# A two-layer conditioned block on one core: LayerNorms of blocks 4 to 7 asked for sooner, one product of the ff residual plain in two blocks, one block's statistics on VectorE, rounds of leaves moved

## The chip, the cores and the metric

The kernel runs on one core of a Trainium2 chip. The metric is device time in microseconds of one execution; the median over several runs is compared. One execution was recorded by the hardware profiler, and all rows of the profile below come from it.

## What is computed

The input is x (2 batches of 2048 tokens of 512 features) and a condition vector per batch. Cut to what matters, the reference is:

```python
emb = silu(t) @ ada_w + ada_b
shift_msa, scale_msa, gate_msa, shift_mlp, scale_mlp, gate_mlp = split(emb, 6)
norm = ln(x) * (1 + scale_msa) + shift_msa
h = gelu(norm @ ssm_w1 + ssm_b1)                  # 512 x 512
x = x + gate_msa * (h @ ssm_w2 + ssm_b2)          # 512 x 512
norm2 = ln(x) * (1 + scale_mlp) + shift_mlp
hf = gelu_tanh(norm2 @ ff_w1 + ff_b1)             # 512 x 1024
x = x + gate_mlp * (hf @ ff_w2 + ff_b2)           # 1024 x 512
```

All of it is fp32.

## The kernel before

The 4096 tokens are cut into 8 blocks of 512. In the first half of the program the blocks run one by one through norm1 (LayerNorm, transposed, modulated), ssm1 (first product with its gelu), ssm2 (second product, gated residual) and norm2 (LayerNorm of the result, transposed, kept in DRAM). In the second half they run in pairs s = 0 to 3: ff1 s for two blocks at once, then ff2 for each of them.

**Products by seven.** Every large product is done by Strassen's scheme in Winograd's form: the operands are cut into quarters, sums of quarters are formed on VectorE and POOL (`first`, `second`, L420 and L430), and seven products P1 to P7 take the place of eight; the results are added up in PSUM and by VectorE. One product of ssm1 or ssm2 (`product`, L771) is four matmuls of 256 columns. ff1 uses the scheme twice, one inside the other. In ff2 and in parts of ssm2 some of the seven products are themselves done by seven smaller ones, called leaves: a leaf of ff2 is two matmuls of 128 columns, a leaf of ssm2's head one. A product that isn't cut in leaves is called plain here.

**The head of ssm2 and its rounds.** P1 and P5 of ssm2 are done by leaves, and ahead of the rest: their matmuls stand between the products of the next block's ssm1. `head` (L697) makes four rounds. Round 0 seeds two PSUM banks with the bias, runs the leaves P1 and P5 of both products, and has ScalarE copy the results aside; round 1 runs leaves P6 and P2 and has VectorE add; round 2 runs P7 and has VectorE add; round 3 runs P4 and P3. With round 1 go two sums that later leaves need (`with_late`, L760). `HEAD_AT` (L694) names the products of ssm1 behind which the rounds stand. ssm1's own order is `CARRIED` (L445): P1, P5, P6, P2, P7, P3, P4. There are six such heads, for blocks 1 to 6, in ssm1 2 to ssm1 7; block 7's head stands in ssm2 6 and has its own list, `LAST_HEAD_AT`.

**P6 of ff2.** In ff2 (`ff2`, L1114) P6 is done by leaves if its leaf operands are among `wops` (`sixth`, L1211: four steps spread over the chain's rounds, with ScalarE copies, POOL adds and VectorE adds beside 14 matmuls), and else in one piece in chain round 4 (`plain_sixth`, L1204: eight matmuls of 256 columns). `fw2_sixth` (L934) makes the weight's leaf operands by four sums, one of which overwrites a quarter of the plain operand.

**norm1.** `norm1` (L629) loads a block of x (1 MB), takes mean and variance (`stats`, L516, on VectorE), makes the scales by eight small operations on POOL (`scales`, L551), normalises on ScalarE and transposes on VectorE in four slices through two small buffers, writes the transposed rows to DRAM in four DMAs, loads them back rearranged in one (blocks 3 to 7), modulates them on ScalarE in four pieces, and forms the four sums that ssm1 needs (`norm1_sums`, on VectorE or POOL). Blocks 4 to 7 are asked for in the loop at L1417, three blocks ahead.

**norm2's statistics.** For the blocks in `STATS_BY_ACT` (L526), norm2 takes the statistics on ScalarE, by eight activations with an accumulated sum (`act_sum`, L528); for the others by `stats` on VectorE.

**Who sets the order.** Nothing is issued where it is written. Each operation goes into a planner (`Plan`, from L20) with the engines that may do it, a cost and a latency. TensorE's operations keep the order in which they are written. Each gets a due time by summing their costs; from these a latest time (`late`) is worked out backwards for every other operation:

```python
late = min(late, ops[s].late - (1 + op.care) * (self.HOP + min(op.lat.values()) + op.size / self.RATE))
```

Here HOP is 70 ns and RATE 370 bytes per ns. `care` is the value of `plan.care` when the operation was added. Then the planner simulates the engines: each takes, of the operations whose inputs are there, the one with the earliest latest time. A large DMA is taken to land after

```python
pipe = max(start + self.FLIGHT, pipe) + op.size / self.RATE * (1 + self.RATED * op.care)
op.end = pipe + self.LANDING + self.LANDED * op.care
```

with RATED 0.5 and LANDED 4000 ns. The order that comes out is fixed when the kernel is built: each engine, and SP's DMA queue, works through its own list and waits at the head of it. So an edit of a latest time can reorder every engine's list. Almost all DMAs are issued on SP's queue.

Of the kernel before, what the change touches and what calls it, by code (L numbers as in the profile page):

```python
# [198 lines left out]
def kernel(  # L199
# [35 lines left out]
    plan = Plan(nc)  # L235
# [287 lines left out]
            plan.add("v", lambda E, st=st, dst=dst: E.bn_aggr(dst, st), [dst], [st], {"v": 100}, {"v": 182})  # L523
        return t, mv

    STATS_BY_ACT = (2, 4, 5)  # L526

    def act_sum(o, a, func, total, bias, scale):  # L528
        ptrs = [] if isinstance(bias, float) else [bias]
# [69 lines left out]
    def next_blocks():  # L599
        turns[0] += 1  # L600
        return blocks[turns[0] % 2]
# [9 lines left out]
    def normed(src, dst, bl, by_act=False):  # L611
        t, mv = stats_by_act(src, banks[2]) if by_act else stats(src)
        rstd, nmr = scales(t, mv)
        for c in range(C):
            normal(dst, src, c, rstd, nmr)
            turn(bl, dst, c)
        return cut(bl, "p (m r) -> p m r", m=C)
# [7 lines left out]
    def turned_out(to, bl):  # L625
        for a in range(C):
            dma(to[:, a].rearrange("(m q) r -> q m r", m=C), bl[a * G : (a + 1) * G])

    def norm1(i):  # L629
        plan.stage = f"norm1 {i}"  # L630
        load_x(i)
        bl = normed(xs[i], passing, next_blocks())
        if i in turned1_d:
            turned_out(turned1_d[i], bl)
            dma(turned[i], turned1_d[i])
        else:
            move(turned[i], bl)
        for k in range(KD):
            modulate(turned[i], k, 0, i // PER_B)
        return norm1_sums(i)  # L640
# [38 lines left out]
    def norm2(i):  # L679
        plan.stage = f"norm2 {i}"  # L680
        turned_out(turned_d[i], normed(xs[i], passing if i else xs[i], next_blocks(), i in STATS_BY_ACT))

# [8 lines left out]
        stages[0] += 1  # L691
        return bank_set()

    HEAD_AT, LAST_HEAD_AT = ("P5", "P2", "P7", "P3"), ("P6", "P2", "P7", "P3")  # L694
    SECOND_BY_LEAVES = (1, 2, 3, 4, 5, 6, 7)

    def head(stage, leaves, seeds, at=HEAD_AT):  # L697
# [41 lines left out]
    def second_leaves(wops):  # L739
        plan.stage = "leaves of w2"  # L740
        return {p: second(halves_of(wops[p]), w2_l[n]) for n, p in enumerate(("P1", "P5"))}

    def second_head(i, ops):
        if i not in SECOND_BY_LEAVES:
            return {}
        plan.stage = f"ssm2 {i}"
        row, leaves = gb2[i // PER_B], {}
        lates = []
        for n, p in enumerate(("P1", "P5")):
            still = first(crossed(ops[p]), hidden_l[i >= PER_B][n])  # L750
            lates.append(still)
            leaves[p] = lambda f, p=p, still=still: (still[f], w2_leaves[0][p][f])

        def seeds(n, bank):
            copy(bank[:, HT:], row[:, n * HT : (n + 1) * HT])

        at = LAST_HEAD_AT if i + 1 == NBLK else HEAD_AT
        rounds = head(f"ssm2 {i}", leaves, seeds, at)

        def with_late(fn):  # L760
            fn()
            for o in lates:
                tt("vg", o["P2"], o["P2"], o["P6"], ALU.subtract)

        rounds[at[1]] = lambda fn=rounds[at[1]]: with_late(fn)
        return rounds
# [71 lines left out]
    def ssm2(i, ops, wops, order=CARRIED, hooks={}):  # L838
        plan.stage = f"ssm2 {i}"
        b = next_set()  # L840
        row = gb2[i // PER_B]
        xt, F = xs[i], D // 2
        q = {"P2": xt[:, 0:2, :F], "P6": xt[:, 0:2, F:], "P3": xt[:, 0:2, F:], "P4": xt[:, 2:4, :F]}
        q["P1"], q["P5"] = q["P2"], xt[:, 2:4, F:]
        q["P7"] = q["P5"]
        if i in SECOND_BY_LEAVES:
            order = AFTER_HEAD
            copy(pair(b["x"]), pair(b["y"]))
            tt("v", q["P5"], pair(b["v"]), q["P5"], ALU.add)
        else:  # L850
            seed(b["y"], row, 0)
            seed(b["v"], row, 1)
        for p in order:
            product(
                b[BANK[p]],
                p,
                lambda j, k: ops[p][:, k, j * P : (j + 1) * P],
                lambda j, k: wops[p][:, k, :],
                KD // 2,
                p == "P2" and order is PLAIN,  # L860
            )
            if p == "P1" and order is CARRIED:
                copy(pair(b["x"]), pair(b["y"]))
            else:
                tt("v", q[p], pair(b[BANK[p]]), q[p], ALU.add)
            between(hooks, p, f"ssm2 {i}")
        for h in range(2):
            dma(x1_d[i][:, 2 * h : 2 * h + 2], xt[:, 2 * h : 2 * h + 2])
# [6 lines left out]
    def quarter_row(b):  # L875
        t = cut(gb2[b], "p (h e d) -> p h e d", h=2, e=2)
        tt("vg", t[:, :, 1], t[:, :, 1], t[:, :, 0], ALU.subtract)

    def weight2(b, bank):
        plan.stage = f"weight2 {b}"  # L880
        t = w2_t[b]
        load_w(t, w2)
        g = gate(2, b, bank)
        gate_bias(gb2[b], g, b2)
        for k in range(KD):
            tt("v", t[:, k, :], t[:, k, :], g, ALU.mult)
        return second(quarters_of_second(t, KD), thirds(w2_s), cuts=1)
# [33 lines left out]
    def leaves_of(w, at):  # L921
        return second({n: v[:, :, 0, :] for n, v in leaf_views(w).items()}, thirds(fw2_l[:, at]))
# [11 lines left out]
    def fw2_sixth(plain, leaves):  # L934
        leaves["P6"] = leaves_of(plain, 6)

    def weight_fw2(b, bank):
        plan.stage = f"weight_fw2 {b}"
        for n in range(2):
            for o in range(2):  # L940
                dma(fw2_t[:, 4 * n + 2 * o : 4 * n + 2 * o + 2], fw2_source()[n, o], lead=100000.0)
        g = gate(5, b, bank)
        gate_bias(gb5, g, fb2)
        for n in range(2):
            lo, hi = [gb5[:, (2 * n + e) * P : (2 * n + e + 1) * P] for e in range(2)]
            tt("vg", hi, hi, lo, ALU.subtract)
        for k in range(KH):
            tt("v" if bank else "vg", fw2_t[:, k, :], fw2_t[:, k, :], g, ALU.mult)
        return fw2_operands()
# [29 lines left out]
    def weight_fw2_loaded(b):  # L979
        plan.stage = f"weight_fw2 {b}"  # L980
        for n in range(4):
            dma(fw2_t[:, 2 * n : 2 * n + 2], fw2_d[:, 2 * n : 2 * n + 2])
        for n in range(3):
            dma(fw2_s[:, n], fw2_sd[:, n])
        load_row(gb5, gb5_d)
        q, t = quarters_of_second(fw2_t, KH), thirds(fw2_s)
        return fw2_operands({"P1": q["11"], "P2": q["21"], "P3": q["22"], "P4": t[2], "P5": t[0], "P6": t[1], "P7": q["12"]})
# [14 lines left out]
    def normed2(i):  # L1002
        plan.stage = f"tokens {i}"
        t = turned2[i % 2]
        if i in SOON:
            for a in range(C):
                dma(t[:, a], turned_d[i][:, a])
        else:
            dma(t, x1_d[i])
            move(t, normed(t, t, kb(far_r, 0, 8)))  # L1010
        for k in range(KD):
            modulate(t, k, 3, i // PER_B)
# [403 lines left out]
    weight_fw1()  # L1416
    for i in range(1, NBLK):  # L1417
        if i + 3 < NBLK:
            plan.care = 0.2
            tok[i + 3] = norm1(i + 3)  # L1420
            plan.care = 0.45
        last = i + 2 >= NBLK
        hooks = second_head(i + 1, hid[i + 1]) if last and i + 1 < NBLK else {}
        ssm2(i, hid[i], w2_ops, CARRIED, hooks)
        if i in SOON:
            norm2(i)
        if i == 4:
            ff = weight_fw2(0, 1)
            fw2_sixth(*ff)
        if i + 1 == PER_B:  # L1430
            w2_ops = weight2(1, 1)
            quarter_row(1)
            w2_leaves[0] = second_leaves(w2_ops)
        if not last:
            hid[i + 2] = ssm1(i + 2, tok[i + 2], w1_ops, second_head(i + 1, hid[i + 1]))
    for s in range(NBLK // 2):
        if 2 * s == PER_B:
            ff = weight_fw2_loaded(1)
            fw2_sixth(*ff)
        if 2 * s + 2 == PER_B:  # L1440
            weight_fw2_ahead(1)
        ff1(s)
        if 2 * s + 2 < NBLK and 2 * s + 2 not in SOON:
            normed2(2 * s + 2)
        for blk in range(2):
            ff2(s, blk, *ff)
# [51 lines left out]
```

## Time and profile before

| what | value |
|---|---|
| median of 3 runs | 568.27 us (567.67 to 569.56) |
| the profiled execution | 569.21 us, of which its span 567.4 us |
| ssm1 4 begins (norm1 4 needed) | 107.48 us |
| ssm1 7 begins (norm1 7 needed) | 180.19 us |
| ff1 0 begins | 216.7 us |
| ff2 0 and ff2 1 | 259.4 to 303.4 us |

Rows name a line (L294 is the matmul of `mm`, L256 the two-tensor operation of `tt`, L274 an activation, L283 a copy on ScalarE, L316 a DMA), the engine, the operation and the tiles written and read. The tiles are named by their regions: `turned` holds transposed tokens, `hidden` ssm1's and ff1's results, `rows`, `ring` and `far` blocks of x among others, `near` weights, `fw` ff weights, `bank` PSUM. PE is TensorE, PEld its weight loads, DVE VectorE, ACT ScalarE, POOL GpSimd, SPq the queue of DMAs. Since the program's order is known, a row can be matched to its stage.

### The profile page before, as it was taken

The page shows a single profiled execution, that of the slowest core. Times are in us where ns is not written, and L with a number is a line of the kernel's source. Part 1 is how long each engine was busy: PE and PEld are TensorE (multiplying, and loading weights), DVE is VectorE, ACT ScalarE, POOL GpSimd, SP SyncE. Part 2 cuts the span into 40 slices and gives each one's busy share as a digit, 9 for nine tenths or more (in the row PEclk, how much of TensorE's full clock was granted, in tenths as well). Part 3 has the DMA queues.
Part 4 walks back from the last instruction along what each step waited for, and adds up shares of the span by engine and source line. Part 5 has one row for each costly group of instructions (what it writes and reads, how often), then busy time and mean ns, then how long its engine had stood idle before and what let it go on. Part 6 is the DMA issues. An engine that isn't in the chain of part 4 may idle for free.

```text
span 567.4 us, 10428 instructions
## 1 busy us (share of the span) xinstructions
PE 559.0 (99%) x3577; PEld 506.5 (89%) x3577; DVE 489.0 (86%) x918; ACT 271.8 (48%) x558; POOL 384.1 (68%) x523
## 2 busy tenths in 40 slices
PE   8999999899999999999999999999999999999997
PEld 4888889788897988889999889999889999888997
DVE  5696988799886988989989889999999898789785
ACT  3464856777685875659112356222266222335120
POOL 2887547598934598994767897667795685446660
PEclk9999999999999999999999999999999999999999
DMA  8954899987899867896054889168955041820022
GB/s 314 399 217 90 246 360 277 320 299 264 258 310 307 270 217 220 276 317 217 20 186 152 304 279 342 68 205 274 319 174 207 2 150 43 273 93 29 1 75 74
DMA packets 53057, 119.85 MB, mean 211 GB/s; under 512 B 5473, under 2 KB 10509, under 8 KB 51470
## 3 DMA queue, kind: packets, MB, share of 16 engines
q1 hardware_dynamic: 51842, 118.66, 62.6%
q8 instruction: 28, 0.46, 0.4%
q10 hardware_dynamic: 1164, 0.55, 0.3%
q14 instruction: 23, 0.19, 0.1%
HBM read 77.63 MB, written 40.51 MB: 208 GB/s over the span
## 4 chain that ended last, share of the span: by engine, by line
PE 89%; DMA 6%; DVE 2%; ACT 1%; SPq 1%; issue 0%; DVEq 0%; ACTq 0%
PE bank L294 89%; DMA turned<-turned 3%; DMA turned<-far 2%; DMA fw<-in_L_cond_ada_w_dram 1%; SPq L316 1%; DVE far L591 1%; PE bank L304 0%; DVE rows L256 0%; ACT hidden L274 0%; ACT turned L274 0%; ACT near L274 0%; DVE marks L522 0%; ACT bank L283 0%; DVE ring L256 0%; DVE turned L656 0%
## 5 line engine op out<-in xcount | busy, mean ns | idle before, releaser
L294 PE MATMUL bank<-turned,ring 128*128 128x256 f32 x896 | 209.1, 380 | 1.2 <-ACT turned L274 1.0
L294 PEld LDWEIGHTS bank<-turned,ring 128*128 128x128 f32 x896 | 167.3, 190 | 24.8 <-ACT turned L274 1.8
L256 DVE TENSOR_TENSOR hidden<-bank,hidden 128x512 f32<-128x512 f32 (+1 forms) x171 | 124.8, 755 | 26.9 <-PE bank L294 23.5
L294 PE MATMUL bank<-near,hidden 128*128 128x256 f32 (+1 forms) x470 | 95.6, 350 | 1.8 <-DVE rows L256 1.8
L294 PEld LDWEIGHTS bank<-near,hidden 128*128 128x128 f32 x470 | 82.1, 190 | 11.8 <-DVE rows L256 2.6
L294 PE MATMUL bank<-fw,hidden 128*128 128x128 f32 x640 | 91.0, 276 | 0.0
L256 DVE TENSOR_TENSOR rows<-bank,rows 128x128 f32<-128x128 f32 (+3 forms) x154 | 78.8, 555 | 9.4 <-PE bank L294 8.8
L294 PE MATMUL bank<-ring 128*128 128x256 f32 x336 | 82.5, 381 | 0.0
L294 PEld LDWEIGHTS bank<-fw,hidden 128*128 128x128 f32 x640 | 81.3, 192 | 0.5
L283 ACT COPY bank<-bank 128x512 f32<-128x512 f32 (+2 forms) x88 | 37.2, 424 | 78.0 <-PE bank L294 77.2
L294 PEld LDWEIGHTS bank<-ring 128*128 128x128 f32 x336 | 63.2, 190 | 10.9 <-issue 2.1
L256 POOL TENSOR_TENSOR turned<-turned 128x512 f32<-128x512 f32 (+1 forms) x58 | 63.8, 1114 | 13.2 <-ACT turned L274 6.7
L294 PE MATMUL bank<-fw,far 128*128 128x128 f32 (+1 forms) x656 | 67.4, 275 | 0.1
L256 POOL TENSOR_TENSOR hidden<-hidden 128x128 f32<-128x128 f32 (+2 forms) x52 | 45.6, 881 | 28.8 <-DVE hidden L256 13.5
L274 ACT ACTIVATE hidden<-hidden,cols 128x512 f32<-128x512 f32 (+1 forms) x66 | 44.9, 711 | 38.4 <-DVE hidden L256 38.3
L294 PEld LDWEIGHTS bank<-fw,far 128*128 128x128 f32 (+1 forms) x656 | 61.2, 168 | 1.7 <-issue 1.3
L294 PE MATMUL bank<-fw,near 128*128 128x128 f32 x464 | 61.0, 275 | 0.0
L294 PEld LDWEIGHTS bank<-fw,near 128*128 128x128 f32 x464 | 56.4, 192 | 0.0
L256 POOL TENSOR_TENSOR fw<-fw 128x256 f32<-128x256 f32 (+1 forms) x51 | 42.0, 838 | 14.8 <-DVE turned L256 7.9
L274 ACT ACTIVATE turned<-turned,mod,mod 128x512 f32<-128x512 f32 x56 | 41.9, 805 | 15.5 <-DMA turned<-turned 14.8
L256 DVE TENSOR_TENSOR hidden<-hidden 128x512 f32<-128x512 f32 (+2 forms) x58 | 37.7, 665 | 1.9 <-POOL hidden L256 1.3
L256 POOL TENSOR_TENSOR ring<-turned,ring 128x256 f32<-128x256 f32 x40 | 29.7, 752 | 12.4 <-PE bank L294 6.4
(141 smaller groups left out, 710.2 us busy)
## 6 DMA issues: line engine op xcount, KB each, us to landing
ring<-fw_parts SPq DMA_DIRECT2D x28, 512.0 KB
turned<-far SPq DMA_DIRECT2D x52, 256.0 KB
ring<-fw_parts SPq DMA_DIRECT2D x28, 384.0 KB
rows<-x SPq DMA_DIRECT2D x32, 256.0 KB
turned<-turned SPq DMA_DIRECT2D x32, 256.0 KB
out_dram<-rows SPq DMA_DIRECT2D x28, 256.0 KB
fw_parts<-fw SPq DMA_DIRECT2D x21, 256.0 KB
fw<-in_L_cond_ada_w_dram SPq DMA_DIRECT2D x5, 1024.0 KB
```

The source lines that it names most:

```text
L256: lambda E: E.tensor_tensor(o, a, b, f),
L274: lambda E: E.activation(o, a, func, bias=bias, scale=scale),
L283: plan.add("a", lambda E: E.copy(o, a), [o], [a], {"a": cost}, {"a": cost + 60})
L294: lambda E: E.matmul(o, lhsT, rhs, start=start, stop=stop, skip_group_check=True, **kw),
L316: plan.add(q, lambda E: E.dma_start(out=o, in_=a), outs, ins, {q: plan.ISSUE}, {q: lat}, size=size, lead=lead)
L591: plan.add("v", lambda E: E.transpose(o, a), [o], [a], {"v": 636}, {"v": 705})
```

## The change

Four things are edited:

- Block 2 leaves `STATS_BY_ACT`: its norm2 statistics go from ScalarE to VectorE.
- `HEAD_AT` becomes P5, P6, P2, P3: rounds 1 and 2 of the six heads stand behind P6 and P2 of ssm1 in place of P2 and P7; rounds 0 and 3 stay behind P5 and P3.
- The operations of norm1 4 to norm1 7 are added with a care of 0.45 in place of 0.2.
- `fw2_sixth` for the first batch is called ahead of s = 1 in place of block 4's turn in the first half. So ff2 0 and ff2 1 find no leaf operands for P6 and do it plain; the leaf operands are made later, for ff2 2 and ff2 3.

```diff
-    STATS_BY_ACT = (2, 4, 5)
+    STATS_BY_ACT = (4, 5)
...
-    HEAD_AT, LAST_HEAD_AT = ("P5", "P2", "P7", "P3"), ("P6", "P2", "P7", "P3")
+    HEAD_AT, LAST_HEAD_AT = ("P5", "P6", "P2", "P3"), ("P6", "P2", "P7", "P3")
...
         if i + 3 < NBLK:
-            plan.care = 0.2
+            plan.care = 0.45
             tok[i + 3] = norm1(i + 3)
             plan.care = 0.45
...
         if i == 4:
             ff = weight_fw2(0, 1)
-            fw2_sixth(*ff)
...
     for s in range(NBLK // 2):
+        if s == 1:
+            fw2_sixth(*ff)
         if 2 * s == PER_B:
             ff = weight_fw2_loaded(1)
             fw2_sixth(*ff)
```

## The prediction

> **What bounds the kernel now.** I read the page's busy times, then what TensorE waited for, then the two longest of those waits in the timeline and in the chain of work that ended last. The page first: its columns are busy time, share of the span, instructions.
>
> ```profile
> span 567.4 us, 10428 instructions
> PE 559.0 (99%) x3577; PEld 506.5 (89%) x3577; DVE 489.0 (86%) x918; ACT 271.8 (48%) x558; POOL 384.1 (68%) x523
> ```
>
> TensorE is busy 99% of the span, so the change can win only what TensorE waits, and pays in full for any matmul time it adds. All its waits, with their releasers (total, times, longest):
>
> ```profile
> PE bank L294 <- DVE rows L256: 1.8, 2, 1.5
> PE bank L294 <- POOL small L321: 1.3, 1, 1.3
> PE bank L294 <- ACT turned L274: 1.0, 1, 1.0
> PE bank L294 <- DVE turned L656: 0.2, 1, 0.2
> ```
>
> The POOL and L656 rows are the start of the kernel, which no edit touches. The two others are single events. The timeline around them (start, duration, engine, operation, count; in brackets the idle time before it and who ended it):
>
> ```profile
> 99.69 4.48 PE L294 MATMUL bank<-near,hidden 128*128 128x256 f32 x20
> ...
> 103.70 0.69 DVE L256 TENSOR_TENSOR turned<-turned 128x512 f32<-128x512 f32 x1 [2.93 <-ACT turned L274]
> 104.31 1.28 DVE L256 TENSOR_TENSOR rows<-bank,rows 128x512 f32<-128x512 f32 x2
> ...
> 105.65 1.99 PE L294 MATMUL bank<-near,hidden 128*128 128x256 f32 x8 [1.48 <-DVE rows L256]
> ```
>
> ```profile
> 170.39 8.80 PE L294 MATMUL bank<-near,hidden 128*128 128x256 f32 x40
> ...
> 180.19 2.05 PE L294 MATMUL bank<-turned,ring 128*128 128x256 f32 x7 [1.01 <-ACT turned L274]
> ...
> 180.90 1.16 PEld L294 LDWEIGHTS bank<-turned,ring 128*128 128x128 f32 x6 [0.41 <-ACT turned L274]
> ```
>
> The pace of TensorE between waits (every matmul leaves two records, so x16 is two products of four matmuls):
>
> ```profile
> 107.48 3.62 PE L294 MATMUL bank<-turned,ring 128*128 128x256 f32 x16
> 110.93 0.38 PE L294 MATMUL bank<-near,hidden 128*128 128x128 f32 x2
> ...
> 111.83 3.62 PE L294 MATMUL bank<-turned,ring 128*128 128x256 f32 x16
> ```
>
> Eight matmuls of 256 columns take 110.93 - 107.48 = 3.45 us, 0.431 each. So the 10 matmuls from 99.69 would have been followed at 104.00; they were at 105.65: **1.65 us lost**. The 20 from 170.39 end at 179.01, the next came at 180.19, 1.18 lost, and the weight load of the second pair, due at 180.62, started at 180.90, 0.28 more: **1.46 us lost**. Whose fault? At 103.70 a sum of the LayerNormed tokens (turned<-turned) stood at the head of VectorE's queue and waited 2.93 us for ScalarE's modulation; the evictions (rows<-bank) that TensorE needed stood behind it. That block is norm1 4, as ssm1 4 begins at 107.48. At 180.19, ssm1 7 itself lacks its tokens. In the chain, both modulations wait for the same step, the 1 MB reload of the turned rows:
>
> ```profile
> 93.52 8.61 DMA turned<-turned
> ...
> 171.36 7.94 DMA turned<-turned
> 179.30 0.03 issue
> 179.33 0.82 ACT turned L274
> 180.19 0.70 PE bank L294 x2
> ```
>
> The reload takes 8.6 and 7.9 us, and ScalarE starts on the rows as it lands. The reader should see that both losses are late LayerNorms of blocks 4 to 7.
>
> **The change part by part.**
>
> *Care 0.2 to 0.45.* Nothing is added or removed; the planner's latest time of each norm1 step moves. By L104 each step is due (1 + care) x (70 + latency + bytes/370) ahead of the next: sum 758 ns, modulation 866, reload 4904, store 2779 with the code's constants, 9.31 us together, so the store is asked for 0.25 x 9.31 = 2.3 us sooner, the steps before it more. Besides, L167 and L168 expect the reload to land 0.25 x 4000 + 0.125 x 2834 ns = 1.35 us later, so the waiting sum is put that much further back in VectorE's queue. 2.3 + 1.35 = 3.7 us covers the 2.93 us at 103.70, and 2.3 covers the 1.18 + 0.28 at 180.19. Does being asked for sooner make it sooner? Only if priority, not data, held the chain:
>
> ```profile
> 73.00 0.80 ACT L274 ACTIVATE hidden<-fw,marks 128x512 f32<-128x512 f32 x1
> ```
>
> ```profile
> 83.09 0.70 DVE L591 STREAM_TRANSPOSE far<-near 128x512 f32<-128x512 f32 x1
> ```
>
> Block 4's rows were normalised at 73.8 and first transposed at 83.09: over 9 us in which only VectorE's order held them. Block 7's scales are eight small operations on POOL, of which these are the first and the last:
>
> ```profile
> 148.46 0.19 POOL L555 TENSOR_SCALAR marks<-marks 128x4 f32<-128x4 f32 x1
> ```
>
> ```profile
> 155.16 0.53 POOL L568 TENSOR_SCALAR marks<-marks 128x4 f32<-128x4 f32 x1 [0.71 <-DVE hidden L256]
> ```
>
> Seven microseconds, most of it other blocks' sums between them: a queue again. The bounds are a shift of nothing (both losses stay) and the whole 2.3 us; I take the whole, since the 9 and the 7 us lie far above it: **-1.65 - 1.46 = -3.11 us**. What else moves with it: on VectorE each block's statistics and four transposes, on POOL those eight operations, on ScalarE four normalisations and four modulations, on SP the load of x, four stores and the reload. They pass work without a near due time (the sums and stores of ff1's weights, first read by ff1 0 behind the last ssm2), which hides the exchange; if they pass evictions instead, the price is the slower rival below.
>
> *P6 plain in blocks 0 and 1.* Per block chain round 4 gets 8 matmuls of 256 columns for 14 of 128.
>
> ```profile
> 259.40:303.40 44.00, 44.00 (x393) 43.86 (x392) 41.16 (x86) 13.27 (x36) 25.96 (x29) 1.00 0.35 116
> ```
>
> ff2 0 and 1 fill this stretch: 98 matmuls each, 44.00/196 = 0.224 us. 8 x 0.431 - 14 x 0.224 = 3.45 - 3.14 = +0.31 us a block, **+0.62 us** in all, unhidden, as TensorE is busy 44.00 of 44.00 us. What goes with the leaves is work beside TensorE: per block four copies on ScalarE, two adds on POOL, two on VectorE into PSUM, and four operand sums; worth nothing while TensorE bounds. The four weight sums of fw2_sixth move from ahead of ff1 0 to ff1 1's time; the one that works in place must await ff2 1's plain reads and then has all of ff1 1 before its first use. I cost them at nothing; if that cover went, ff2 2 would wait for the last of them, under a microsecond by the fw<-fw row below.
>
> The Trainium skill ("TensorE: Matmul & The Clock Gate", Back-to-back issue gap) says the spacing in a stream of weight loads and matmuls is set by both, about 81 ns at 128 columns and 131 at 512. Between these, an estimate from that page is 98 ns at 256, 1.2 times the narrow one, by which the plain form would be cheaper. The rows above decide against it here: 0.431 to 0.224 is 1.92.
>
> *Block 2's statistics.* ScalarE loses eight activations, VectorE gets four pairs:
>
> ```profile
> L522 DVE BATCH_NORM_STATS2 marks<-rows 128x6 f32<-128x512 f32 x20 | 12.9, 671 | 0.0
> L523 DVE BATCH_NORM_AGGREGATE marks<-marks 128x2 f32<-128x6 f32 x52 | 7.6, 170 | 0.3
> ```
>
> 4 x (0.671 + 0.170) = 3.4 us on VectorE, after ssm2 2 (from 108). The stretches from there, by ssm1 step (length, then busy time of PE, PEld, DVE, ACT, POOL):
>
> ```profile
> 107.40:131.30 23.90, 23.90 (x126) 21.42 (x125) 23.38 (x45) 19.41 (x45) 20.00 (x33) 1.00 0.81 267
> 131.30:155.20 23.90, 23.90 (x126) 21.39 (x126) 21.21 (x46) 15.18 (x29) 21.32 (x42) 1.00 0.87 283
> ```
>
> VectorE has 0.5 us free in the first and 2.7 in the next. But in the first it also does sums for ff1's weights:
>
> ```profile
> 109.52 3.26 DVE L256 TENSOR_TENSOR fw<-fw 128x512 f32<-128x512 f32 x4
> ```
>
> They are read by ff1 0 first, so 3.26 us (0.8 each) can give way to 3.4. Bounds: 0, and 3.4 - 0.5 = 2.9 us if evictions give way instead. I take 0: evictions have the earlier latest times.
>
> *Rounds of leaves.* Same instructions. Round 1, with the two late sums behind it, now follows P6 alone, 1.73 us after round 0 in place of 3.45; round 2 follows P2, again one product; round 3 gets one product more. What round 1 needs is ScalarE's copies of round 0:
>
> ```profile
> 112.08 0.42 ACT L283 COPY bank<-bank 128x128 f32<-128x128 f32 x2
> 112.43 0.43 ACT L283 COPY quads<-bank 128x128 f32<-128x128 f32 x2
> ```
>
> Done at 112.86; round 1 came at 111.83 + 3.45 = 115.28 and would come at 111.83 + 1.73 = 113.56: 0.7 us to spare. Cost 0, up to 0.9 us in each of the six heads if two activations of 0.8 us (as at 73.00) came between; the copies have the earlier latest time, so I take 0.
>
> The sum: -3.11 + 0.62 = -2.49 us. The profiled execution took 569.21 us (span 567.4, 1.8 around it) and would take 566.7; the median of the three runs shown, 568.27, becomes **565.8 us**. A measurement of this kernel can tell about 0.3% (1.7 us), so this is a gain just over it.
>
> **The rivals.**
> - *Half of it.* Only one of the two losses goes: 568.27 + 0.62 - 1.65 or - 1.46, 567.2 or 567.4. For it: the two blocks are held on different engines. Against: one margin serves both.
> - *The reload keeps its time.* It is bound by other traffic, as 8.6 us here and 7.9 there for the same 1 MB suggest, and starting sooner lands no sooner: 568.27 + 0.62 = 568.9. Against: the queueing of 9 and 7 us lies ahead of it, not in it.
> - *Slower.* VectorE's order is fixed when the kernel is built. If the sum of the tokens moves forward in it by 2.3 us while the reload does not, the evictions behind it wait 2.3 us longer in both places: 568.27 + 0.62 + 4.6 = 573.5. It decides when the landing moves less than the sum's place; the 1.35 us speak against.
> - *Wide matmuls are cheap.* TensorE's time per matmul depends little on width, 0.270 us at 256 columns (1.2 x 0.224): 8 x 0.270 - 14 x 0.224 = -0.98 a block, 568.27 - 3.11 - 1.96 = 563.2. That is the page's rule above. The 0.431 speaks against; chance 2 in 100.
>
> **How the numbers follow.** Forecast 53 in 100, by itself 565.0 to 566.6 (low: the 0.28 us below gone too and 0.5 of the spread of the runs, 567.67 to 569.56; high: 0.8 of the 3.11 left); half 19; reload unchanged 11; slower 15; wide matmuls 2. Faster: 53 + 2 = 55. Same: 30. Slower: 15. Leaving out the last two rivals (17), the range is 564.9 to 569.5: the forecast's low end, and 568.9 with 0.6 for that spread. It takes in the 2.9 us bound of the statistics (568.7); the heads' bound of 0.9 six times would lie above it, and stands with the slower case.
>
> ```profile
> 211.44 1.78 PE L294 MATMUL bank<-near,hidden 128*128 128x256 f32 x7 [0.28 <-DVE rows L256]
> ```
>
> **What would show it.** TensorE's waits for DVE rows and ACT turned shrink to this row or to nothing; the reloads of blocks 4 and 7 are issued over 1.5 us sooner against the PE steps they feed; the stretch of ff2 0 and 1 grows by 0.6 us; no wait follows round 0 of a head. Wrong would be: a new wait on a reload of block 5 or 6, VectorE idle ahead of turned<-turned, or evictions late after 108.

## The result and the profile after

The changed kernel takes **566.51 us** (median of 6 runs, 566.47 to 566.59); the kernel before, run beside it, 568.75 us (6 runs, 567.36 to 569.56). The ratio is 0.9963, 95% interval 0.9948 to 0.9979: faster by 0.4%. The profiled execution took 566.59 us, with a span of 564.8. The prediction was 565.8, range 564.9 to 569.5.

First the page of the changed kernel, its busy times (busy us, share of the span, instructions):

```profile
span 564.8 us, 10322 instructions
PE 557.8 (99%) x3553; PEld 506.3 (90%) x3553; DVE 483.1 (86%) x918; ACT 266.0 (47%) x534; POOL 379.0 (67%) x514
```

TensorE is busy 99% of the span, as before, and 1.2 us less. What it waits for (total, times, longest):

```profile
PE bank L294 <- POOL small L321: 1.3, 1, 1.3
PE bank L294 <- DMA fw<-in_L_cond_ada_w_dram: 0.7, 2, 0.4
PE bank L294 <- DVE hidden L256: 0.5, 2, 0.2
PE bank L294 <- DVE rows L256: 0.2, 1, 0.2
PE bank L294 <- DVE turned L656: 0.2, 1, 0.2
```

The rows of POOL small, DMA fw and DVE turned lie in the start of the kernel. The row of ACT turned (1.0) is gone, and DVE rows has shrunk from 1.8 to 0.2, which is the wait that was 0.28 us at 211.44: both waits that the prediction aimed at have gone. New is DVE hidden, two waits of 0.24 us at the ends of ff1 0 and ff1 1. The stretches of the two old waits, in the timeline of the changed kernel:

```profile
98.68 7.29 PE L294 MATMUL bank<-near,hidden 128*128 128x256 f32 x33
105.80 3.62 PE L294 MATMUL bank<-turned,ring 128*128 128x256 f32 x16
...
169.79 7.72 PE L294 MATMUL bank<-near,hidden 128*128 128x256 f32 x35
177.34 3.62 PE L294 MATMUL bank<-turned,ring 128*128 128x256 f32 x16
```

ssm1 4 begins at 105.80 (before 107.48) and ssm1 7 at 177.34 (before 180.19), both without an idle bracket. ff2 0 and ff2 1 (length of the stretch, then busy time of PE, PEld, DVE, ACT, POOL):

```profile
256.30:300.70 44.40, 44.40 (x369) 43.57 (x368) 40.28 (x86) 11.30 (x27) 23.34 (x24) 1.00 0.34 113
```

44.40 us where the row before had 44.00; by the first matmuls of ff2 0 and ff1 1, found from the program's order, 44.42 and 44.07, so 0.36 more. ScalarE and POOL have less to do in it. To split the rest I took, in both traces, the first matmul of ff1 0 and of ff1 2 in the same way: up to ff1 0 216.75 us before and 213.47 after (**-3.28**), from ff1 0 to ff1 2 173.26 and 174.14 (**+0.88**), from there to TensorE's end -0.25. The sum, -2.65, agrees with the spans (567.4 - 564.8 = 2.6). The question that is left is which of the four edits did it.

### The profile page after: what moved, and what is told of

The parts are those of the page before. It is cut to its first block, busy times and chain, and to the rows that moved or that the text cites. A ratio compares the mean times of both kernels' runs of the same rounds, so it can differ in the third digit from the quotient of the medians.

```text
span 564.8 us, 10322 instructions
## 1 busy us (share of the span) xinstructions
PE 557.8 (99%) x3553; PEld 506.3 (90%) x3553; DVE 483.1 (86%) x918; ACT 266.0 (47%) x534; POOL 379.0 (67%) x514
## 4 chain that ended last, share of the span: by engine, by line
PE 94%; DVE 3%; DMA 1%; issue 1%; POOL 0%; SPq 0%; DVEq 0%
PE bank L294 94%; DMA fw<-in_L_cond_ada_w_dram 1%; DVE hidden L256 1%; DVE near L256 0%; DVE marks L522 0%; PE bank L304 0%; POOL hidden L256 0%; POOL near L256 0%; SPq L316 0%; DVE rows L256 0%; DVE ring L256 0%; DVE fw L256 0%; DVE far L591 0%; DVE turned L656 0%; DVE marks L523 0%
## 5 line engine op out<-in xcount | busy, mean ns | idle before, releaser
L294 PE MATMUL bank<-fw,far 128*128 128x128 f32 (+2 forms) x644 | 67.6, 278 | 0.7 <-DMA fw<-in_L_cond_ada_w_dram 0.7
L294 PE MATMUL bank<-fw,near 128*128 128x128 f32 (+1 forms) x452 | 61.1, 279 | 0.0
L256 POOL TENSOR_TENSOR hidden<-hidden 128x128 f32<-128x128 f32 (+2 forms) x52 | 43.6, 847 | 22.6 <-DVE hidden L256 6.4
L256 POOL TENSOR_TENSOR fw<-fw 128x256 f32<-128x256 f32 (+1 forms) x52 | 45.0, 875 | 13.3 <-DVE fw L256 7.7
L256 POOL TENSOR_TENSOR ring<-turned,ring 128x256 f32<-128x256 f32 x37 | 27.8, 757 | 15.8 <-PE bank L294 9.7
L256 DVE TENSOR_TENSOR hidden<-hidden 128x512 f32<-128x512 f32 (+2 forms) x58 | 34.9, 621 | 1.2 <-ACT hidden L274 0.8
```

Of the source, the lines that this page charges most:

```text
L256: lambda E: E.tensor_tensor(o, a, b, f),
L294: lambda E: E.matmul(o, lhsT, rhs, start=start, stop=stop, skip_group_check=True, **kw),
```

## The experiments

Two theories stand against each other at first. **S**, that of the prediction: each edit has its own price (care -3.1, P6 +0.6, the others 0), and prices add up. **J**: an edit counts mainly by how it re-sorts the fixed lists of all engines, so its price depends on the other three. Every kernel was timed against the kernel before on the same chip; the median of before was 568.88, 568.84 and 568.77 us in the three groups of four (28, 24 and 24 runs).

### One edit alone

`only_care`: the loop's care of 0.2 becomes 0.45.

```diff
-            plan.care = 0.2
+            plan.care = 0.45
             tok[i + 3] = norm1(i + 3)
```

> The kernel before with the care of norm1 4 to 7 at 0.45 and nothing else changed. Theory S (each edit does its own work, whatever the others): both late reloads go, 1.65 + 1.46 us, so some 3.1 us less than before, about 565.5, and TensorE has no wait over 0.5 us after the start. Theory J (the edits only work together: any changed latest time reorders every engine's list, and with P6 by leaves in blocks 0 and 1 its sums crowd VectorE and POOL): the wait ahead of ssm1 4 goes, but new waits of 1 to 3 us in all stand at ssm1 7 and in ff2 1, so 567.5 to 569.5, no better than before beyond the noise.

Measured: 571.05 us (5 runs, 570.86 to 571.12), ratio 1.0044 (1.003 to 1.0059). The wait ahead of 105.65 is gone, the one ahead of ssm1 7 is not:

```profile
PE bank L294 <- ACT turned L274: 0.9, 1, 0.9
PE bank L294 <- DVE rows L256: 0.5, 2, 0.3
PE bank L294 <- ACT bank L283: 0.4, 1, 0.4
PE bank L294 <- POOL far L256: 0.4, 1, 0.4
PE bank L294 <- DVE far L256: 0.3, 1, 0.3
```

The two `far` rows are operands of leaves in ff2 1, which takes 23.59 us in place of 22.04. Care alone makes the kernel slower, by more than J had in its range. S falls.

`only_p6`: only the call of `fw2_sixth` moved.

```diff
             ff = weight_fw2(0, 1)
-            fw2_sixth(*ff)
...
     for s in range(NBLK // 2):
+        if s == 1:
+            fw2_sixth(*ff)
```

> The kernel before with P6 of blocks 0 and 1 plain and nothing else changed. Both theories: the late reloads of blocks 4 and 7 stay, and the stretch of ff2 0 and 1 gains 0.3 to 0.6 us; 569 to 569.5 beside a kernel before of 567.4 to 569.6. If the waits of blocks 4 and 7 go here too, both theories are wrong about their cause.

Measured: 569.03 us (12 runs), ratio 1.0007 (0.9993 to 1.0022). ff2 0 and 1 took 44.51 us, 0.45 more than before by the same marks. The wait ahead of ssm1 7 stayed; of the one at 105.65 only 0.36 us of lost time was left (ssm1 3 took 24.21 us over its usual 23.85), and in this execution the same reload took 7.35 us in place of 8.63 and landed at 100.78 in place of 102.15.

`only_stats`: block 2's statistics on VectorE.

```diff
-    STATS_BY_ACT = (2, 4, 5)
+    STATS_BY_ACT = (4, 5)
```

> The kernel before with block 2's statistics moved from ScalarE to VectorE, nothing else. Theory S (each edit does its own work; 3.4 us more on VectorE where it has 0.5 to 2.7 us free per step and sums of ff weights to put off): within 0.5 us of the kernel before, both waits for late tokens (1.48 and 1.01 us) still there. Theory J (an edit acts by re-sorting every engine's list, so that its effect depends on the others): the waits of the first half move, the one ahead of ssm1 7 goes, and new waits of 1 to 2 us each stand in ff2 0, 1 or 3 where P6's leaves take ScalarE, POOL and VectorE; slower than before by 0.5 to 4 us.

Measured: 573.29 us (6 runs, 571.93 to 574.87), ratio 1.0079 (1.0053 to 1.0104). The wait ahead of ssm1 7 is gone (J), the other stands, and ff2 0, 1 and 3 take 24.97, 23.55 and 23.76 us where 22.0 is usual:

```profile
PE bank L294 <- POOL fw L256: 2.4, 1, 2.4
PE bank L294 <- DVE rows L256: 1.6, 2, 1.4
...
PE bank L294 <- DVE far L256: 1.1, 1, 1.1
```

`only_rounds`:

```diff
-    HEAD_AT, LAST_HEAD_AT = ("P5", "P2", "P7", "P3"), ("P6", "P2", "P7", "P3")
+    HEAD_AT, LAST_HEAD_AT = ("P5", "P6", "P2", "P3"), ("P6", "P2", "P7", "P3")
```

> The kernel before with rounds 1 and 2 of the six heads one product sooner, nothing else. Theory S: the same instructions and cover enough, so within 0.5 us of the kernel before, with the waits of 1.48 and 1.01 us kept. Theory J: the lists are re-sorted; some of the two waits changes and ff2 1 gets waits of 2 to 4 us on the operands of P6's leaves, as in the version of the changed kernel that keeps these leaves (4 us): slower by 1 to 4 us.

Measured: 572.04 us (7 runs, 571.2 to 576.11), ratio 1.0074 (1.0046 to 1.0103). ff2 1 takes 25.10 us (J), and heads wait too. Its timelines of ScalarE and TensorE around the head in ssm1 4:

```profile
108.20 0.81 ACT L274 ACTIVATE near<-far,marks 128x512 f32<-128x512 f32 x1 [1.15 <-POOL marks L568]
108.92 0.80 ACT L274 ACTIVATE hidden<-far,marks 128x512 f32<-128x512 f32 x1
109.62 0.36 ACT L283 COPY bank<-fw 128x256 f32<-128x256 f32 x1
```

```profile
110.03 0.49 PE L294 MATMUL bank<-near,hidden 128*128 128x128 f32 x2 [0.62 <-ACT bank L283]
```

The copy that seeds a bank for round 0 stands behind two activations of 0.8 us, and TensorE waits 0.62 us for it. This is the collision that the prediction bounded at 0.9 us and costed at 0, at round 0 instead of round 1.

### Three edits, one left out

These undo the same single edits in the changed kernel; their diffs are the above, reversed.

`no_care`:

> The changed kernel with the care back at 0.2. Theory S: the reloads of blocks 4 and 7 are late again, some 3 us of waits on DVE rows or ACT turned ahead of ssm1 4 and ssm1 7; about 569.5. Theory J: the other three edits have reordered the lists as well, and the late reload may meet them elsewhere or nowhere: anything from 566.3 (no wait over 0.5 us) to 570; if it is under 567.5, care was not what removed the waits.

Measured: 567.14 us (12 runs, 566.22 to 568.39), ratio 0.9972 (0.996 to 0.9983). No wait for turned rows is left in it without any of the new care.

`no_p6`:

> The changed kernel with P6 of blocks 0 and 1 by leaves again (fw2_sixth back in the first half). Theory S: TensorE's work falls by what the plain form cost, 0.4 to 0.8 us: 565.7 to 566.1, the best kernel of all. Theory J: the sums of the sixth product crowd VectorE and POOL ahead of ff2 1, TensorE waits there for some 3 us in all, and the stretch from the start of ff2 0 to the end of ff2 1 grows from 44.4 us to about 47: 568.5 to 569.5.

Measured: 569.77 us (10 runs, 569.15 to 570.31), ratio 1.002 (1.001 to 1.003). Up to ff1 0 its stages have the lengths of the changed kernel's within 0.01 us. The loss stands in ff2 1, which takes 26.22 us; a block of ff2 in leaves that waits for nothing takes 21.89 (ff2 5 of before). TensorE's timeline there, and what the stretches give (before the last two columns, the granted clock):

```profile
280.58 2.12 PE L294 MATMUL bank<-fw,far 128*128 128x128 f32 x12 [1.98 <-POOL far L256]
282.50 1.15 PE L294 MATMUL bank<-fw,hidden 128*128 128x128 f32 x4
```

```profile
278.40:280.50 2.10, 0.20 (x2) 0.01 (x1) 2.10 (x5) 0.38 (x1) 2.10 (x4) 1.00 0.00 0
280.50:282.50 2.00, 1.84 (x13) 1.64 (x13) 2.00 (x4) 0.52 (x2) 1.26 (x2) 0.93 0.47 174
282.50:285.50 3.00, 3.00 (x14) 2.93 (x14) 2.97 (x8) 1.03 (x4) 0.00 (x0) 0.50 0.74 234
285.50:288.50 3.00, 3.00 (x29) 3.00 (x28) 1.78 (x5) 0.90 (x3) 1.23 (x2) 0.98 0.86 273
```

TensorE waits for a sum on POOL. In that stretch POOL (fifth busy time) is busy 2.10 of 2.10 us, and VectorE (third), which could do such a sum too, has the evictions and is full from 278.4 to 285.5. The wait is 1.98 us, the loss 4.3: behind the wait the clock is granted at half for 3 us (14 matmul records in the time in which 29 run at full clock), which is 1.7 us, and 0.6 us is not traced. J had the place right, and too low a price.

`no_stats`:

> The changed kernel with block 2's statistics left on ScalarE. Theory S: 566.5 us as the changed kernel, within 0.5. Theory J: ScalarE's list is as full as before in the steps in which block 7's rows are normalised and modulated, so a wait for turned rows of about 1 us comes back ahead of ssm1 7, with one under 1 us at the start of ff1 0 or in ff2 2: 567.5 to 569.5 us.

Measured: 569.46 us (12 runs, 569.2 to 570.45), ratio 1.0011 (1.0 to 1.0023). Waits came where J had them or near: 0.2 us ahead of ssm1 7 (expected 1), 0.5 at the end of ff1 0 (expected at its start), 0.7 in ff2 2.

```profile
177.62 3.99 PE L294 MATMUL bank<-turned,ring 128*128 128x256 f32 x16 [0.21 <-ACT turned L274]
...
256.54 1.10 PE L294 MATMUL bank<-ring 128*128 128x256 f32 x4 [0.52 <-DVE hidden L256]
...
348.10 1.60 PE L294 MATMUL bank<-fw,near 128*128 128x128 f32 x12 [0.68 <-DVE near L256]
```

`no_rounds`:

> The changed kernel with the heads' rounds where they were (behind P5, P2, P7, P3). Theory S: 566.5 us as the changed kernel, within 0.5. Theory J: waits of about 1 us in ff2 1, ff1 1 or ff2 2 that the changed kernel has not; the two waits of the first half stay away: 567 to 569 us.

Measured: 570.06 us (12 runs, 569.9 to 570.08), ratio 1.0023 (1.001 to 1.0036), 1 us above J's range. The first half is that of the changed kernel (ff1 0 begins at 213.5); the waits stand in ff2 1 (1.19, the stage 23.88 us), ff1 1 (0.42) and ff2 2 (0.68), far from every head.

Alone, then, no edit gains: +2.2, +0.2, +4.5 and +3.2 us for care, P6, statistics and rounds, by the medians against the kernel before of the same group. Left out of four, each costs, against the changed kernel's 566.51: 0.6, 3.3, 3.0 and 3.6 us. J gave the direction and mostly the stage, S failed seven times in eight (P6 alone is between them); which place in which list carries each of these prices isn't settled by that.

### One number of the change, varied

`care05` and `care035` are the changed kernel with another care:

```diff
-            plan.care = 0.45
+            plan.care = 0.5
             tok[i + 3] = norm1(i + 3)
```

> The changed kernel with a care of 0.5 in place of 0.45 for norm1 4 to 7. Theory S (asking sooner is what helps): 566.5 us or up to 0.3 less. Theory J (an edit re-sorts every list, and its result is not monotone in the edit): no wait for tokens in the first half, but new waits of over 1 us each in ff2 0 and ff2 1: 568.5 to 570.5 us.

Measured: 571.99 us (6 runs, 571.27 to 573.23), ratio 1.0072 (1.0052 to 1.0091). A step of 0.05 in one number costs 5.5 us, more than J's 568.5 to 570.5 has room for: waits of 1.25 us in ff2 0, 1.14 in ff2 1, 1.04 in ff2 2 and, in the first half, 0.83 for late evictions at 105.50.

> The changed kernel with a care of 0.35 in place of 0.45. Theory S: between the changed kernel with 0.2 (567.1) and with 0.45 (566.5). Theory J: this value happens to give lists without a wait over 0.3 us: 566.2 to 566.7 us, while its neighbour 0.5 loses.

Measured: 567.7 us (12 runs, 567.26 to 569.67), ratio 0.9988 (0.9976 to 1.0001). Here J named too good a time, and S's 566.5 to 567.1 is missed too: against the changed kernel's stages it lost 0.5 us in ff1 1 and 0.2 to 0.3 each in ssm1 7, ff2 1 and ff1 3, none of it foreseen. 0.2, 0.35, 0.45 and 0.5 give 567.1, 567.7, 566.5 and 572.0 us: no trend, as J has it.

### The list alone, with no edit of the work

Theory **L**: each of the two waits of before was the place of a few operations in a list, and moving just these gives the gain. Theory **T**: the transfer itself is late, and the next operation will wait for it. `sum_later` keeps all lists of before and puts one VectorE operation two places later (operation 707 is norm1 4's first sum, 899 the second of the evictions behind it):

```diff
-    for op in plan.order():
+    key = {op.n: op.start for op in plan.order()}
+    key[707] = key[899] + 1.0
...
+    for op in listed:
```

> The kernel before with its lists frozen and one operation moved: norm1 4's sum on VectorE (the one that waited 2.93 us at 103.70) stands behind the two evictions that it held up; one POOL sum of ssm1 3 that was tied behind it is tied no more. Theory L (the loss is the place of that one sum; the reload need not be sooner): the reload still goes out near 93.5 and lands near 102, and the 1.65 us ahead of 105.65 are gone while the loss ahead of ssm1 7 stays: 1.2 to 1.7 us faster than before. Theory T (the late reload is the loss, and the sum only shows it): TensorE waits at ssm1 4 instead, for modulated tokens or for norm1 4's sums on POOL: within 0.5 us of before.

Measured: 568.01 us (12 runs, 567.19 to 569.2), ratio 0.9995 (0.9982 to 1.0008). Its VectorE and TensorE (line numbers are one higher in this kernel):

```profile
101.81 1.43 DVE L257 TENSOR_TENSOR rows<-bank,rows 128x512 f32<-128x512 f32 x2
103.16 0.68 DVE L257 TENSOR_TENSOR turned<-turned 128x512 f32<-128x512 f32 x1
```

```profile
97.81 8.15 PE L295 MATMUL bank<-near,hidden 128*128 128x256 f32 x37
105.80 2.54 PE L295 MATMUL bank<-turned,ring 128*128 128x256 f32 x11
```

The evictions pass, TensorE runs through, and ssm1 4 doesn't wait in its turn. The reload landed at 100.94 here, 1.2 us sooner than in the trace of before, so this trace alone can't tell the two theories apart; the next kernel can. The gain over many runs is 0.8 us by the medians, in an interval from 1.0 us faster to 0.5 slower: it isn't clear of zero, and not the 1.2 to 1.7 of L. The profiled execution of before, with 569.21 us and a reload of 8.63, probably showed more of this wait than a usual run has (`only_p6`, with the same lists up to here, lost 0.36); 0.37 us was also given back in ff2 2 (22.32 us against 21.95).

`sum_and_chain` also puts norm1 7's statistics, scales, normalisations, transposes and stores 3 us sooner in the lists:

```diff
+    for n in range(1214, 1242):
+        key[n] -= 3000.0
```

> As the version with norm1 4's sum moved, and also norm1 7's statistics, scales, normalisations, transposes and stores put 3 us sooner in the frozen lists of their engines, with nothing of care, statistics, rounds or P6 changed. Theory L: norm1 7's reload goes out 2 to 4 us sooner against ssm1 7, the wait there (1.46 us) goes too: 2.6 to 3.2 us faster than before, so 565.6 to 566.3 us, as fast as the changed kernel or up to 0.8 us faster, as P6 keeps its leaves at no wait. If the run-to-run spread of before (over 2 us) comes from the landing of these two reloads, it shrinks to some tenths. Theory T: the queue or the memory holds the reload, it lands no sooner: like the version with the sum alone. A loss is possible where the 30 operations put ahead hold up evictions: then a new wait for DVE rows between 140 and 165.

Measured: 570.69 us (7 runs, 569.85 to 571.39), ratio 1.0041 (1.0024 to 1.0058): slower, against both theories' main case. The first wait, though, it settles: its reload of block 4 landed at 101.91, almost as late as in before, and TensorE runs through to ssm1 4:

```profile
97.16 8.80 PE L295 MATMUL bank<-near,hidden 128*128 128x256 f32 x40
105.79 3.62 PE L295 MATMUL bank<-turned,ring 128*128 128x256 f32 x16
```

Up to here the lists of before, `only_p6`, `only_stats` and these two are the same but for the moved sum. With the sum in its old place, landings at 102.15, 100.78 and 102.06 lost 1.74, 0.36 and 1.67 us ahead of ssm1 4; with the sum moved, landings at 100.94 and 101.91 lost nothing. So T fails for this wait: a late transfer cost TensorE time only through the sum at the head of VectorE's queue.

What makes this kernel slower is a new wait, in its VectorE and TensorE:

```profile
137.25 0.70 DVE L523 BATCH_NORM_STATS2 marks<-rows 128x6 f32<-128x512 f32 x1 [2.52 <-DMA rows<-in_x_dram]
```

```profile
142.20 0.68 PE L295 MATMUL bank<-near,hidden 128*128 128x128 f32 x4 [0.98 <-DVE bank L257]
```

norm1 7's first statistics stand at the head of VectorE's queue and wait 2.52 us for block 7's rows, whose load goes out at 130.31, not much sooner than before (131.01). The head's additions stand behind them; ssm1 5 takes 26.93 us in place of 23.85; and the reload goes out at 173.51, later than before (171.36). What holds norm1 7 back is further up: its load.

### What holds norm1 7's load

Block 7's rows go into the buffer of block 2's, which is free when norm2 2 has normalised its last slice. In before that is ScalarE's work behind the eight activations of norm2 2's statistics. First and last of them, the last normalisation, and SP's load:

```profile
108.30 0.59 ACT L533 ACTIVATE bank<-rows 128x512 f32<-128x512 f32 x1
...
118.12 0.69 ACT L533 ACTIVATE bank<-rows,marks 128x512 f32<-128x512 f32 x1
...
130.14 0.80 ACT L274 ACTIVATE hidden<-rows,marks 128x512 f32<-128x512 f32 x1
```

```profile
131.01 0.38 SPq L316 DMA_DIRECT2D rows<-in_x_dram  x1
```

In the changed kernel VectorE takes these statistics at once:

```profile
107.00 1.28 DVE L522 BATCH_NORM_STATS2 marks<-rows 128x6 f32<-128x512 f32 x2
...
109.17 0.18 DVE L523 BATCH_NORM_AGGREGATE marks<-marks 128x2 f32<-128x6 f32 x1
```

```profile
120.76 0.80 ACT L274 ACTIVATE hidden<-rows,marks 128x512 f32<-128x512 f32 x1
```

```profile
126.22 0.37 SPq L316 DMA_DIRECT2D rows<-in_x_dram  x1
...
161.60 0.58 SPq L316 DMA_DIRECT2D turned<-turned  x1
```

The statistics are done at 109.35 in place of 118.81, the buffer is free at 121.56 in place of 130.94, the load goes out 4.8 us sooner and the reload 9.8 us sooner. The same points in the traces (us from the span's start; the landing is the start of the first modulation; `sum_and_chain` is left out, as ssm1 5 delays everything behind it):

| kernel | block 2's statistics on | buffer free | reload of block 7 lands | lost ahead of ssm1 7 |
|---|---|---|---|---|
| before | ScalarE | 130.94 | 179.33 | 1.17 |
| `only_care` | ScalarE | 128.50 | 177.99 | 1.42 |
| `only_p6` | ScalarE | 129.57 | 178.37 | 1.58 |
| `only_rounds` | ScalarE | 133.71 | 178.79 | 0.76 |
| `sum_later` | ScalarE | 129.28 | 177.73 | 1.23 |
| `no_stats` | ScalarE | 128.56 | 176.75 | 0.37 |
| `only_stats` | VectorE | 125.14 | 176.11 | 0 |
| `no_care` | VectorE | 124.55 | 176.31 | 0 |
| `no_rounds` | VectorE | 123.41 | 171.91 | 0 |
| `care05` | VectorE | 128.28 | 175.92 | 0 |
| `care035` | VectorE | 128.91 | 176.25 | 0 |
| after | VectorE | 121.56 | 169.64 | 0 |

Lost is the length from the start of ssm1 6 to that of ssm1 7 over its usual 23.85 us. The last column divides by the statistics: on VectorE nothing is lost there, on ScalarE always something. That the buffer is the way by which they act is read from the traces of before and the changed kernel, and no run changes the buffer alone: with it free at 128.3 to 128.9, `care05` and `care035` land in time and `only_care` and `no_stats` don't, so the lists behind the load count too. What sorts all twelve kernels is how long before ssm1 7 is due (23.85 us behind ssm1 6) the reload goes out: 6.9 to 8.2 us where something is lost, 8.5 to 15.7 where nothing is. `no_stats` with 8.2 and `no_care` with 8.5 lie close together, so that the statistics' place decides there only by a little.

## Why the prediction was right, and where not

**The two waits and their size: right.** The stages of the two waits became 1.74 and 1.17 us shorter, against 1.65 and 1.18 forecast, and ssm1 7 itself 0.43 us shorter, of which 0.28 were forecast; the total is -2.65 us against -2.49. The end time is 0.7 us above the forecast: the sum was made on the profiled execution (569.21 to 566.59, -2.62) and taken off a median of 568.27, and a median run of before has about 0.9 us less to lose than the profiled one, while every run of the changed kernel lies within 0.12 us of its profiled one. That the total fits so well is partly luck: the forecast gave both waits to one edit, took two others at 0, and none of the three wins anything alone. (The low end of the range, called the forecast's, should have been 565.0; nothing hangs on it.)

**"I take the whole, since the 9 and the 7 us lie far above it: -1.65 - 1.46 = -3.11 us", put to care's account: wrong.** Care alone is 2.2 us slower, and the other three edits without it give 567.14 us, 1.6 of the 2.2 us. Care alone does remove the first wait, but not by making the reload sooner: in the changed kernel block 4's goes out at 94.82 against 93.52, so the named sign of 1.5 us failed for it. The step that failed is the reading that only VectorE's order held block 4's rows for 9 us. They are transposed into a buffer that still holds norm2 0's rows until four stores of these have landed, and in the changed kernel VectorE stands and waits for that:

```profile
81.44 0.71 DVE L591 STREAM_TRANSPOSE far<-near 128x512 f32<-128x512 f32 x1 [2.04 <-DMA turned<-far]
```

In before the last of these stores landed at 81.26 (from the DMA semaphores of the trace) and the first transpose came at 83.09, so at most some 2 of the 9 us were VectorE's order, and for the rest the buffer was not free. In all fourteen kernels block 4's last transpose ends between 86.07 and 86.80, whatever the care. What care alone did change, against before, is the place of norm1 4's first sum. The prediction had a second reason for that, the landing expected later, which was to put the sum further back in VectorE's queue; instead it leaves this queue for POOL, as in the changed kernel:

```profile
102.03 2.92 ACT L274 ACTIVATE turned<-turned,mod,mod 128x512 f32<-128x512 f32 x4
...
104.77 1.27 POOL L256 TENSOR_TENSOR turned<-turned 128x512 f32<-128x512 f32 x1
```

The rows land at 102.03, as late as before (102.15), and no eviction stands behind them. Which term of the planner moves the sum wasn't separated: with a care of 0.2 the first sum stayed on VectorE in before, `only_p6` and `only_stats`, but not in `no_care` and `only_rounds`, so other edits move it too.

For block 7 the mechanism held, but only in company: its reload goes out 15.7 us before ssm1 7 is due in the changed kernel and 8.5 in `no_care`, while care alone gives 7.95 in place of before's 7.66, and the wait stays. In the changed kernel this is margin beyond what the wait needed, as `no_care` has no wait there either.

**"Block 2's statistics ... I take 0": wrong, and this is the step that failed for the second wait.** It prices the eight activations as work on an engine with room. Their price was in their place: ahead of the normalisation that frees the buffer for block 7's load. Moving them is what removed the second wait (`only_stats` against before, `no_stats` against the changed kernel, and the table). By itself it then loses more than that, 4.5 us, in ff2 and at the first wait.

**P6: the term was right, its neighbour wrong.** A block of ff2 in leaves with no wait takes 21.89 us (ff2 5 in before), a plain-P6 block 22.21 (ff2 0 and 1 after): +0.32 against +0.31 worked out. The stretch grew by 0.36 and not 0.62 since before lost some tenths there to small waits. (By the rule of the Trainium skill's page "TensorE: Matmul & The Clock Gate", Back-to-back issue gap, as the prediction estimated from it, plain P6 would have been 0.98 us cheaper a block; the trace disagrees.) But "worth nothing while TensorE bounds" failed: with the leaves kept, POOL and VectorE are full at the start of ff2 1 (`no_p6`), and TensorE waits 1.98 us there and loses 4.3. There the work beside the bound engine was free only up to the point at which its own engines were full.

**Rounds at 0: right for the heads in this kernel**, where no wait follows a round, and wrong for the whole, as the changed kernel without this edit is 3.6 us slower. `only_rounds` shows a 0.62 us wait at a head where ScalarE was occupied by other activations. How the rounds' place leads to waits in ff2 1, ff1 1 and ff2 2, 100 us later, stays open; that all four edits re-sort VectorE's and POOL's lists is as far as the runs go.

**The rivals.** The reload takes 7.2 us for block 4 and 8.0 for block 7, against 8.6 and 7.9. Block 7's, sent 9.8 us sooner, landed 9.7 us sooner, so that rival is out for it; block 4's wasn't sent sooner. The slower one (a moved operation at the head of a queue holds up what stands behind it) isn't what the whole change did, but it is what `sum_and_chain` did, at 2.52 us of VectorE's time and 1.9 us of the whole. "One margin serves both" against *half of it* was mistaken: the two waits have different causes, and each edit alone that removed one left the other or brought new ones.

No version tried beats the changed kernel.

## What to carry to other kernels

Where a planner fixes all queues, don't add up the prices of edits: run the combination, and each edit left out of it, since four edits of which three lose 2.2 to 4.5 us alone, and none gains, win 2.2 together. For a late transfer, follow the chain up to what frees its buffer before looking at the queues in it: the operation to move may be another block's, here some 50 us ahead of that transfer. A dependent operation at the head of an in-order queue costs what stands behind it, so moving it later, or to another engine, can do as much as making its data come sooner.

## What the runs showed of the hardware

A short wait of TensorE cost nearly twice its length here. Behind the 1.98 us in `no_p6` the clock was granted at 0.93, 0.50 and 0.98 for 2, 3 and 3 us, which by itself is 0.14 + 1.5 + 0.06 = 1.7 us more; behind the 2.4 us in `only_stats` it fell to 0.50 as well:

```profile
284.80:285.80 1.00, 1.00 (x7) 1.00 (x7) 1.00 (x2) 0.24 (x1) 0.80 (x1) 0.50 0.00 0
```

Behind the 1.48 us of before, the 1.42 and 1.41 of `only_p6` and `only_stats`, and the 1.25 and 1.14 of `care05` it stayed at 1.00. The Trainium skill ("TensorE: Matmul & The Clock Gate", Part 1: The HAM clock gate) puts the fall behind an idle window of about 3.4 us; here 1.98 us was enough.

The same 1 MB reload took, for blocks 4 and 7, between 5.54 us (block 7 in `no_rounds`) and 8.63 us (block 4 in before) from issue to the first use. For block 4 it took 6.54 to 8.63 us in five kernels whose DMA lists agree up to there (`sum_later`, `only_p6`, `sum_and_chain`, `only_stats` and before).

Whether the margin in front of ssm1 7 makes the runs even stays open. For it: 565.96 to 571.53 us over 76 runs of before, whose reload of block 7 comes too late; 566.22 to 568.39 for `no_care`, where it lands 1.3 us ahead of ssm1 7; 569.9 to 570.08 and 566.47 to 566.59 for `no_rounds` and the changed kernel, where it lands over 5 us ahead. Against it: `only_care`, whose reload comes too late, has its five runs within 570.86 to 571.12, and `no_p6`, with the margin of the changed kernel, spreads from 569.15 to 570.31.
